# Per-token scalars of two graph layers turned by VectorE and spread by transfers instead of by a TensorE product

## The chip, the cores and the metric

The kernel runs on one core of a Trainium2 chip. A core has a matmul engine (TensorE, PE in the profile; its weight loads are PEld), three engines for elementwise work (VectorE or DVE, ScalarE or ACT, GpSimd or POOL) and SyncE (SP), which only issues transfers here; ScalarE issues some transfers too. Each engine works its own instructions in order and waits for the others by semaphores. The metric is the device time of one launch in microseconds, the median of several runs. Before the change it is 2524.32 us (three runs, 2521.54 to 2528.27).

## The reference

Four graph layers are applied to x, 128 graphs of 64 nodes with 512 features, float32. Each is `x + layer(relu(layernorm(x)))`. Biases, the node mask (all ones) and layers 1 and 2 (attention inside each graph, with one head and with eight) are cut here to what the change meets:

```python
# layer 0
q, k = jnp.split(h @ Wqk, 2, axis=-1)
v = h @ Wv
agg = jnp.einsum('bij,bjd->bid', adj, k)
w = jnp.einsum('bid,bid->bi', q, agg) / jnp.sqrt(512.)    # one scalar a node
x = x + jax.nn.softmax(w, axis=1)[:, :, None] * v         # over the 64 nodes of a graph

# layer 3
Xw = X @ Wv + bv
sj = Xw @ aw[:d, 0]                                       # one scalar a node
si = Xw @ aw[d:, 0]                                       # one scalar a node
e = jax.nn.leaky_relu(sj[:, None, :] + si[:, :, None] + ab[0], negative_slope=0.2)
alpha = A * jnp.exp(e)
transition = alpha / (jnp.sum(alpha, axis=-1, keepdims=True) + 1e-12)
H, Xk = 0, X
for k in range(3):
    H = H + Xk @ Wk[k] + bk[k]
    Xk = jnp.einsum('bij,bjd->bid', transition, Xk)
x = x + relu(H)
```

In both layers a scalar that belongs to a node must be known to all nodes of its graph: w for the softmax, si for the sum with sj. How it gets there is what is changed.

## The kernel before

**Tiles.** A block is 256 tokens, four graphs: two tiles (t = 0, 1) of 128 tokens, one token a partition, two graphs a tile. There are 32 blocks. Every 512x512 product over a block is done with seven products of half-size operands (Strassen's scheme) instead of eight. POOL forms the sums S of the turned input hT (L270 to L274), PE the products (`Product.add`, L299 or L306 in the trace). Products 1 and 6 go first, 5 and 4 second, 2, 7 and 3 late, into two banks, ab and dc. After the first ones ACT keeps p1 and DVE u2 (`keep_ab`, L335 and L336), after the second ACT keeps p5 (`keep_dc`, L344); only then may PE go on in the same bank with the late ones. `store` (L358 to L362) adds it up into the result; the bank is free for the next product when DVE has read it there: ab after L359, dc after L361. In the trace names such as u_y, p_y, ab_y belong to a product y; layer 3 has three, y2 and y1 (the head) and y0 (the tail), and the trace leaves their numbers out.

**Norm.** `norm` (L180) takes DVE's statistics (L185, L186, L188, L189), POOL's rstd and nmr (L191, L193) and ACT's h (L200, two halves, each followed by a transfer to a scratch in DRAM, L204, that ACT issues itself). SP reads it back in another order (L217) and DVE turns it into hT by 32x32 squares (L243).

**The scalars.** In layer 0 DVE's dot (L609) gives w, one value a token, in a column. L616 multiplies an identity of 64 columns by it (wd), so that each row holds w on its own place, and `graph_sums` (L453) multiplies the result by a matrix of two 64x64 blocks of ones on PE (L457): each row of the product, sm_w in PSUM, holds the w of all 64 nodes of its graph. `layer0_end` takes its min (L627), the exponentials on ACT (L633, L638) and updates x (L643). In layer 3 `layer3_dots` does four dots (L915: si and sj, each for two tiles), the multiplication by the identity (L920) and sj (L927); `layer3_in` has the product (sm_i), adds sj (L934), and makes al from it (L940, ACT's exp L941, L943).

**Order.** The program order is written by hand: steps hand lists of closures (`between`) to the places between the first, second and late products, and `tc.issue_after` puts instructions right behind a named one in the order of their own engines. What is issued later on one engine waits behind what is issued earlier.

- Layers 0 and 1 run interleaved, two blocks of layer 0 and two of layer 1 in four steps (the loop over `steps`). `layer0_end` of a block is put in the first slot of the next step, `chore` (L100 to L104, sums of later layers' weights on POOL) in the second.
- Layer 2 runs block by block, fed by `prepare2` and `fetch2`, with the norm and the dots of the first blocks of layer 3 at its end.
- Layer 3 (`layer3_step`): in step b the head does y2 and y1, with the sums and the turn of b + 1 and the norm of b + 2 placed early (behind the last `kept_ab`), `layer3_end` of b - 1 in the second slot (PE's po, L449, then ACT's tz L1013, POOL's L1015, DVE's L1016 and the store of the output), and `layer3_in` of b + 1 in the third. The tail does y0, with den (L966, the row sums of al) and po2, whose results DVE scales at L974 to L977; y0 is stored at L1000 to L1004, and behind its end (`kept`) come the dots of b + 2 and the loads of b + 3.

Of the kernel before, what the change touches and what calls it, by code (L numbers as in the profile page):

```python
# [26 lines left out]
def kernel(ctx: ExitStack, tc: tile.TileContext, a: dict, out: bass.AP):  # L27
# [72 lines left out]
    def chore(n: int = 1):  # L100
        with tc.issue_after(behind[0].ins):
            for _ in range(min(n, len(chores))):
                w, (to, x, y) = chores.pop(0)
                nc.gpsimd.tensor_tensor(w[:, to], w[:, x], w[:, y], ALU.subtract)  # L104
# [63 lines left out]
    eye = const.tile([P, N], FP, tag="eye", name="eye")  # L168
    for g in range(2):
        h = slice(g * N, (g + 1) * N)  # L170
        nc.vector.memset(ones_bd[h, h], 1.0)
        nc.vector.tensor_copy(eye[h, :], ident[h, h])
# [4 lines left out]
    behind_norm, parted = {}, {}  # L177
    read, w2 = [None], []

    def norm(x, name: str, home):  # L180
# [13 lines left out]
        behind_norm.setdefault(0, (by_rows, summed_up))  # L194
        h = med.tile([P, TT, D], FP, tag="h", name=f"h_{name}", bufs=homes["h"])
# [60 lines left out]
    behind = [None]  # L256
# [21 lines left out]
    class Product:  # L278
# [77 lines left out]
        def store(self, y):  # L356
# [4 lines left out]
            nc.vector.tensor_tensor(y[:, 0, F:], self.c, self.u2, ALU.add)  # L361
            nc.gpsimd.tensor_tensor(y[:, 1, F:], self.u3, self.p5, ALU.add)  # L362
# [91 lines left out]
    def graph_sums(e, cols: int, name: str):  # L454

        ps = ps_sc.tile([P, cols], FP, tag="sc", name=f"sm_{name}")
        nc.tensor.matmul(ps, ones_bd, e, start=True, stop=True)  # L457
        return ps

    def reciprocals(e, name: str):  # L460

        den = graph_sums(e.rearrange("p t i -> p (t i)"), TT * N, name)
        r = small.tile([P, TT, N], FP, tag="r", name=f"r_{name}", bufs=2)
        nc.vector.reciprocal(r.rearrange("p t i -> p (t i)"), den)
        return r
# [56 lines left out]
    def setup1():  # L522
# [43 lines left out]
        folded(kt, qt, 1, m, lambda: layer0_end(0, *softmax))  # L566
# [29 lines left out]
    def layer0(b: int, x, adjT, hs, hT, aggs, between):  # L596
# [10 lines left out]
        w = small.tile([P, TT], FP, tag="w", name=f"w_{b}")  # L607
        for t in range(TT):
            nc.vector.scalar_tensor_tensor(  # L609
# [3 lines left out]


        wd = small.tile([P, TT, N], FP, tag="e", name=f"wd_{b}")
        tail[0] = nc.vector.tensor_tensor(  # L616
            wd,
            eye.unsqueeze(1).to_broadcast([P, TT, N]),
            w.unsqueeze(2).to_broadcast([P, TT, N]),
            ALU.mult,  # L620
        )
        return x, gv, w, wd

    def layer0_end(b: int, x, gv, w, wd):
        wrow = graph_sums(wd.rearrange("p t i -> p (t i)"), TT * N, f"w_{b}")
        mn = small.tile([P, TT], FP, tag="mx0", name=f"mn0_{b}")
        nc.vector.tensor_reduce(  # L627
            mn, wrow.rearrange("p (t i) -> p t i", t=TT), AX.X, ALU.min
        )
        nc.vector.tensor_tensor(w, w, mn, ALU.subtract)  # L630
        tot = small.tile([P, TT], FP, tag="tot", name=f"tot_{b}")
        for t in range(TT):
            nc.scalar.activation(  # L633
                wd[:, t, :], wrow[:, t * N : (t + 1) * N], AF.Exp, bias=mn[:, t : t + 1],
                scale=-1.0, accum_out=tot[:, t : t + 1],
            )
# [270 lines left out]
    def layer3_dots(b: int, x, adjT, hs):  # L907
# [3 lines left out]
        sij = small.tile([P, 2, TT], FP, tag="sij", name=f"sij_{b}")  # L911
        for s in range(2):
            for t in range(TT):
                hu = med.tile([P, D], FP, tag="agg", name=f"hu_{b}_{s}_{t}", bufs=2)
                nc.vector.scalar_tensor_tensor(  # L915
                    hu, hs[t], 1.0, us[s], ALU.mult, ALU.mult,
                    accum_out=sij[:, s, t : t + 1],
                )
        di = small.tile([P, TT, N], FP, tag="e", name=f"di_{b}")
        nc.vector.tensor_tensor(  # L920
            di,
            eye.unsqueeze(1).to_broadcast([P, TT, N]),
            sij[:, 1, :].unsqueeze(2).to_broadcast([P, TT, N]),
            ALU.mult,
        )
        sj = small.tile([P, TT], FP, tag="sj", name=f"sj_{b}")
        nc.vector.tensor_scalar(sj, sij[:, 0, :], c3, None, ALU.add)  # L927
        return x, adjT, hs, di, sj

    def layer3_in(b: int, x, adjT, hs, e, sj, made: dict):  # L930


        pi = graph_sums(e.rearrange("p t i -> p (t i)"), TT * N, f"i_{b}")
        nc.vector.tensor_tensor(  # L934
            e,
            pi.rearrange("p (t i) -> p t i", t=TT),
# [188 lines left out]
    for i, (layer, b) in enumerate(steps):  # L1125
        if i == n_steps - 4:
            fetch2(0)
        if i == n_steps - 3:
            fetch2(1)
        if i == n_steps - 1:  # L1130
            fetch2(2)
        between = [[], [lambda: chore(3 if i < 4 else 1)], []]
        if i == 1:
            begun = []
# [18 lines left out]
        elif i + 2 == n_steps:  # L1153
            between[0].append(lambda: prepare2(0))
        else:
            between[0].append(lambda: prepare2(1))
        if layer == 0:
            softmax = layer0(b, *loaded[b], *normed[i], aggs.pop(b, None), between)
            begun = [(0, lambda b=b, softmax=softmax: layer0_end(b, *softmax))]
# [23 lines left out]
    def layer3_step(b: int, ahead: bool = True):  # L1183
# [8 lines left out]
        def begin():  # L1192
# [3 lines left out]
            if b + 2 < n_blk and ahead:  # L1196
                with tc.issue_after(kept_ab[0].ins):
                    normed3 = layer3_norm(b + 2)

        def attention():  # L1200
            if b + 1 < n_blk:
                layer3_in(b + 1, *coming, made_in)

        y = layer3_head(b, ops, [[begin], [ending.pop()], [attention]])
# [7 lines left out]
        if b + 1 == n_blk:  # L1212
            ending[0] = lambda: layer3_last(b, x, al, y, r, y0, ops, kept)
        if b + 2 < n_blk:
            with tc.issue_after(kept.ins):
                if ahead:
                    normed3 = layer3_dots(b + 2, *normed3)
                    fetch3(b + 3)
                else:
                    fetch3(b + 2)  # L1220
# [17 lines left out]
    for b in range(n_blk):  # L1238
        x = loaded2[b][0]
        first_in = lambda: layer3_in(0, *normed3, made_in) if b == n_blk - 2 else None  # L1240
        if b + 1 < n_blk:
            pTs = []
# [5 lines left out]
            def ahead():  # L1248
                with ExitStack() as placed:
                    for i in (pTs[1], kept_c[0], read[0]):  # L1250
                        placed.enter_context(tc.issue_after(i.ins))
                    prepare2(b + 3)
                with tc.issue_after(read[0].ins):
# [121 lines left out]
```

## Time and profile before

One profiled execution, on the same kind of core:

| | us |
|---|---|
| median of three runs | 2524.32 |
| profiled execution, its own time | 2527.11 |
| its span, first to last instruction | 2524.5 |
| PE busy (19488 instructions) | 2487.0 |
| DVE busy (4590) | 1822.0 |
| POOL busy (1710) | 1324.1 |
| ACT busy (2106) | 857.1 |

The time lies 2.6 us above the span, for what lies around it. By time the layers are: the setup to about 110, layers 0 and 1 to about 900, layer 2 to about 1800, layer 3 from there to the end. Most instructions of a group are alike, and a group's row gives their sum and the mean of one. A wait is given as "engine, what it was to do, what it waited for". A busy PE means that matmuls follow each other: the ends of matmuls are modelled, so what a matmul costs is best read from one start to the next.

The transfers that matter here, by their mean time from issue to landing: h to DRAM 2.1 us (256 KB), the parts back 2.8 us (128 KB each), x 3.7 us (512 KB), adjT 2.2 us (64 KB).

### The profile page before, as it was taken

The page shows a single profiled execution, that of the slowest core. Times are in us where ns is not written, and L with a number is a line of the kernel's source. Part 1 is how long each engine was busy: PE and PEld are TensorE (multiplying, and loading weights), DVE is VectorE, ACT ScalarE, POOL GpSimd, SP SyncE. Part 2 cuts the span into 40 slices and gives each one's busy share as a digit, 9 for nine tenths or more (in the row PEclk, how much of TensorE's full clock was granted, in tenths as well). Part 3 has the DMA queues.
Part 4 walks back from the last instruction along what each step waited for, and adds up shares of the span by engine and source line. Part 5 has one row for each costly group of instructions (what it writes and reads, how often), then busy time and mean ns, then how long its engine had stood idle before and what let it go on. Part 6 is the DMA issues. An engine that isn't in the chain of part 4 may idle for free.

```text
span 2524.5 us, 52284 instructions
## 1 busy us (share of the span) xinstructions
PE 2487.0 (99%) x19488; PEld 2124.1 (84%) x19488; DVE 1822.0 (72%) x4590; ACT 857.1 (34%) x2106; POOL 1324.1 (52%) x1710
## 2 busy tenths in 40 slices
PE   9899999999999999999999999999989999999999
PEld 5788888888888888999999999999867777777776
DVE  5577777777777786667667667667568777777775
ACT  3333433333334332333333333333223333333332
POOL 2444343444433445666656556556465555555554
PEclk9999999999999999999999999999999999999999
DMA  7344343333343354443343343344433333333320
GB/s 180 94 127 124 111 127 114 119 107 116 113 126 112 122 156 138 128 133 108 122 132 115 123 131 115 122 136 134 139 112 104 104 103 107 105 106 106 103 77 34
DMA packets 305190, 295.50 MB, mean 117 GB/s; under 512 B 56870, under 2 KB 211494, under 8 KB 304936
## 3 DMA queue, kind: packets, MB, share of 16 engines
q1 hardware_dynamic: 258856, 208.26, 29.2%
q10 hardware_dynamic: 46080, 83.91, 9.1%
q8 instruction: 153, 2.51, 0.4%
q14 instruction: 101, 0.83, 0.1%
HBM read 158.91 MB, written 133.18 MB: 116 GB/s over the span
## 4 chain that ended last, share of the span: by engine, by line
PE 57%; DVE 2%; DMA 1%; POOL 1%; issue 1%; SPq 0%; ACT 0%; POOLq 0%; ACTq 0%; DVEq 0%
PE ab_y L306 13%; PE dc_y L306 9%; PE ab_v L306 4%; PE ab_q L299 4%; PE ab_k L299 4%; PE ab_o L306 4%; PE dc_q L299 3%; PE dc_k L299 3%; PE dc_v L306 3%; PE dc_o L306 3%; PE po L449 2%; PE pc L825 1%; PE s L750 1%; DVE hu L915 1%; DMA x<-x 0%
## 5 line engine op out<-in xcount | busy, mean ns | idle before, releaser
L200 ACT ACTIVATE h<-x,nmr,rstd 128x512 f32<-128x512 f32 x256 | 194.8, 806 | 207.6 <-POOL nmr L193 202.1
L270 POOL TENSOR_TENSOR S<-hT 128x256 f32<-128x256 f32 x128 | 97.8, 764 | 243.9 <-DVE hT L243 231.1
L306 PE MATMUL ab_y<-L_Wk,hT 128*128 128x256 f32 x768 | 204.9, 389 | 7.9 <-DVE u_y L336 6.7
L306 PE MATMUL ab_v<-L_Wv,hT 128*128 128x256 f32 x768 | 201.0, 384 | 3.7 <-DVE u_v L336 3.0
L306 PEld LDWEIGHTS ab_y<-L_Wk,hT 128*128 128x128 f32 x768 | 138.7, 190 | 74.9 <-DVE u_y L336 30.7
L191 POOL TENSOR_TENSOR rstd<-ve,neghalf 128x2 f32<-128x2 f32 x128 | 90.5, 707 | 209.2 <-DVE mv L189 190.7
L306 PE MATMUL dc_v<-L_Wv,S 128*128 128x256 f32 x768 | 198.0, 380 | 0.7 <-ACT p_v L344 0.7
L306 PE MATMUL ab_y<-L_Wk,S 128*128 128x256 f32 x768 | 198.0, 380 | 0.0
L306 PE MATMUL ab_v<-L_Wv,S 128*128 128x256 f32 x768 | 197.1, 379 | 0.0
L306 PE MATMUL dc_y<-L_Wk,S 128*128 128x256 f32 x768 | 193.5, 380 | 0.1
L243 DVE STREAM_TRANSPOSE hT<-part 128x512 f32<-128x512 f32 x252 | 174.4, 698 | 8.6 <-DMA part<-h_rows 5.9
L306 PEld LDWEIGHTS dc_y<-L_Wk,S 128*128 128x128 f32 x768 | 146.0, 191 | 21.3 <-issue 0.8
L306 PEld LDWEIGHTS ab_y<-L_Wk,S 128*128 128x128 f32 x768 | 146.5, 191 | 20.1
L185 DVE BATCH_NORM_STATS2 stats<-x 128x6 f32<-128x512 f32 x256 | 162.8, 677 | 0.0
L306 PEld LDWEIGHTS ab_v<-L_Wv,S 128*128 128x128 f32 x768 | 145.9, 190 | 19.8
L306 PEld LDWEIGHTS dc_v<-L_Wv,S 128*128 128x128 f32 x768 | 143.8, 191 | 20.0 <-ACT p_v L344 0.9
L306 PEld LDWEIGHTS ab_v<-L_Wv,hT 128*128 128x128 f32 x768 | 138.2, 190 | 21.9 <-DVE u_v L336 4.0
L915 DVE SCALAR_TENSOR_TENSOR hu<-h,us 128x512 f32<-128x512 f32 x128 | 139.4, 1139 | 1.9 <-POOL bs L894 1.4
L1015 POOL TENSOR_TENSOR tz<-tz,y 128x512 f32<-128x512 f32 x62 | 90.4, 1458 | 95.4 <-ACT tz L1013 95.3
L336 DVE TENSOR_TENSOR u_v<-ab_v,p_v 128x256 f32<-128x256 f32 x96 | 40.4, 421 | 126.4 <-ACT p_v L335 125.9
L1016 DVE SCALAR_TENSOR_TENSOR x<-tz,x 128x512 f32<-128x512 f32 x62 | 42.9, 692 | 112.3 <-POOL tz L1015 112.3
L272 POOL TENSOR_TENSOR S<-hT,S 128x256 f32<-128x256 f32 x128 | 113.0, 883 | 0.0
(257 smaller groups left out, 6181.7 us busy)
## 6 DMA issues: line engine op xcount, KB each, us to landing
x<-x SPq DMA_DIRECT2D x128, 512.0 KB, 3.8
h_rows<-h ACTq DMA_DIRECT2D x252, 256.0 KB, 2.1
part<-h_rows SPq DMA_DIRECT2D x504, 128.0 KB, 2.8
x<-in_x_dram SPq DMA_DIRECT2D x32, 512.0 KB, 3.7
e_rows<-et ACTq DMA_DIRECT2D x64, 256.0 KB, 3.0
pT<-e_rows SPq DMA_DIRECT2D x128, 128.0 KB, 3.1
out_dram<-x SPq DMA_DIRECT2D x31, 512.0 KB, 2.8
adjT<-in_adjT_dram SPq DMA_DIRECT2D x64, 64.0 KB, 2.2
```

Source lines behind the costliest of these rows:

```text
L185: nc.vector.bn_stats(stats[:, t, :], x[:, t, :])
L191: nc.gpsimd.tensor_tensor(rstd, ve, neghalf, ALU.pow)
L200: nc.scalar.activation(hs[t], x[:, t, :], AF.Relu, bias=nmr[:, t : t + 1], scale=rstd[:, t : t + 1])
L243: nc.vector.transpose(hT[:, :, t * P : (t + 1) * P].rearrange("p k (g q) -> p g k q", q=Q), part[:, t * 4 : (t + 1) * 4].rearrange("p g (k ...
L270: nc.gpsimd.tensor_tensor(S1, A21, A22, ALU.add)
L272: nc.gpsimd.tensor_tensor(S4, A12, S2, ALU.subtract)
L299: nc.tensor.matmul(dst[:, m * P : (m + 1) * P], w[:, place, k, m * P : (m + 1) * P], left[:, k, :], start=key not in self.begun, stop=last ...
L306: nc.tensor.matmul(dst, left[:, k, :], w[:, place, k, :], start=key not in self.begun, stop=last and k == 1, skip_group_check=True,)
L449: nc.tensor.matmul(ps[t][half[g ^ t]], e[half[g], t, :], us[t][half[g]], start=True, stop=True)
L915: nc.vector.scalar_tensor_tensor(hu, hs[t], 1.0, us[s], ALU.mult, ALU.mult, accum_out=sij[:, s, t : t + 1],)
L1015: nc.gpsimd.tensor_tensor(tz[t], tz[t], y0[:, t, :], ALU.add)
L1016: nc.vector.scalar_tensor_tensor(x[:, t, :], tz[t], 0.0, x[:, t, :], ALU.max, ALU.add)
```

## The change

The identity, the two multiplications by it (L616, L920) and `graph_sums` are taken out. In their place the column of scalars is written into a 128x32 tile that is zero elsewhere (two of them, by turns); DVE turns it by 32x32 squares, so that the scalars lie in rows; SP writes these rows to a scratch in DRAM (two transfers) and reads them back to all 64 partitions of each graph (two transfers).

```diff
-    def graph_sums(e, cols: int, name: str):
-
-        ps = ps_sc.tile([P, cols], FP, tag="sc", name=f"sm_{name}")
-        nc.tensor.matmul(ps, ones_bd, e, start=True, stop=True)
-        return ps
...
+    def spread(pair, name: str):
+
+        row = tc.dram_tile([TT, P], FP, name=f"{name}_row")
+        lines = small.tile([P, Q], FP, tag="lines", name=f"{name}_lines", bufs=2)
+        nc.vector.transpose(lines, pair)
+        for t in range(TT):
+            nc.sync.dma_start(
+                row[t : t + 1].rearrange("o (s q) -> (o s) q", q=Q), lines[t::Q]
+            )
+        to = small.tile([P, TT, N], FP, tag="e", name=name)
+        by_graph = row.rearrange("(o t) (g i) -> g o t i", o=1, g=2)
+        for g in range(2):
+            spread_out[0] = nc.sync.dma_start(
+                to[half[g]], by_graph[g].to_broadcast([N, TT, N])
+            )
+        return to
```

The users read this tile in SBUF instead of the product in PSUM, and later:

```diff
 # layer 0
-        wd = small.tile([P, TT, N], FP, tag="e", name=f"wd_{b}")
-        tail[0] = nc.vector.tensor_tensor(
-            wd,
-            eye.unsqueeze(1).to_broadcast([P, TT, N]),
-            w.unsqueeze(2).to_broadcast([P, TT, N]),
-            ALU.mult,
-        )
-        return x, gv, w, wd
+        return x, gv, w, spread(pair, f"w_of_{b}")
...
-        wrow = graph_sums(wd.rearrange("p t i -> p (t i)"), TT * N, f"w_{b}")
-        nc.vector.tensor_reduce(
-            mn, wrow.rearrange("p (t i) -> p t i", t=TT), AX.X, ALU.min
-        )
+        nc.vector.tensor_reduce(mn, wd, AX.X, ALU.min)
...
-            begun = [(0, lambda b=b, softmax=softmax: layer0_end(b, *softmax))]
+            def end0(b=b, softmax=softmax):
+                with tc.issue_after(stored[1].ins):
+                    layer0_end(b, *softmax)
+
+            begun = [(3, end0)]
 # layer 3
+        di = spread(pair, f"si_of_{b}")
+        nc.vector.tensor_scalar(sj, sj, c3, None, ALU.add)
...
-        pi = graph_sums(e.rearrange("p t i -> p (t i)"), TT * N, f"i_{b}")
         nc.vector.tensor_tensor(
             e,
-            pi.rearrange("p (t i) -> p t i", t=TT),
+            e,
             sj.unsqueeze(2).to_broadcast([P, TT, N]),
             ALU.add,
         )
...
             if b + 2 < n_blk and ahead:
-                with tc.issue_after(kept_ab[0].ins):
+                with tc.issue_after(kept_ab[0].ins), tc.issue_after(spread_out[0].ins):
                     normed3 = layer3_norm(b + 2)
 
         def attention():
-            if b + 1 < n_blk:
-                layer3_in(b + 1, *coming, made_in)
-
-        y = layer3_head(b, ops, [[begin], [ending.pop()], [attention]])
+            layer3_in(b + 1, *coming, made_in)
+
+        y = layer3_head(b, ops, [[begin], [ending.pop()]])
...
+        if b + 1 < n_blk:
+            with tc.issue_after(kept.ins):
+                attention()
         if b + 2 < n_blk:
             with tc.issue_after(kept.ins):
                 if ahead:
                     normed3 = layer3_dots(b + 2, *normed3)
-                    fetch3(b + 3)
+                    with tc.issue_after(read[0].ins):
+                        fetch3(b + 3)
```

So in layer 0 the min, the exponentials and the update of x are issued behind the store of the second product of the next step. In layer 3 the sum with sj and what follows it moves from between the late products of the head to the end of the step before, ahead of the dots; and the norm of b + 2 is issued behind the spread of the scalars of the block before it.

The rest concerns order alone. POOL's weight sums are also placed behind the first product's store and behind the latest norm:

```diff
-        between = [[], [lambda: chore(3 if i < 4 else 1)], []]
+        between = [[], [
+            lambda: chore(3 if i < 4 else 1, (stored[0], normalised[0]) if i else ())
+        ], [], []]
```

At the seam from layer 1 to 2, x of the first three blocks of layer 2 is loaded in steps n - 6, n - 4 and n - 2 (it was n - 4, n - 3 and n - 1), and `prepare2` of blocks 0 and 1 is placed behind the last dot of layer 0. At the seam from layer 2 to 3, the norms and dots of blocks 0 and 1 of layer 3 are placed in earlier places of layer 2's blocks n - 3 and n - 2, the last block's attention weights are turned and `layer3_in` of block 0 is issued right behind the output product of block n - 2, the loads of x of layer 3 are issued earlier, and the biases later:

```diff
+        if b == n_blk - 2:
+            with tc.issue_after(read[0].ins):
+                fetch3(2)
+                fetch3(3)
+            with tc.issue_after(of_o.taken.ins):
+                pTs = layer2_turned(b + 1, es)
+                layer3_in(0, *normed3_0, made_in)
+            with tc.issue_after(read[0].ins):
+                bias3 = biases3()
```

## The prediction

> **What bounds the kernel now.** I read the busy time of the engines by stretch of the span first, because a mean over four layers hides where there is room. Columns: the stretch in us, its length, then the busy us (and instructions) of TensorE (PE), weight loads, VectorE (DVE), ScalarE (ACT), GpSimd (POOL), then the granted clock, DMA share, GB/s.
>
> ```profile
> 0.00:110.00 110.00, 95.92 (x399) 67.36 (x400) 59.66 (x152) 38.89 (x87) 39.27 (x60) 0.97 0.57 148
> 110.00:860.00 750.00, 746.70 (x5305) 640.14 (x5305) 558.22 (x1498) 285.98 (x747) 312.96 (x461) 1.00 0.39 116
> 1740.00:1900.00 160.00, 148.58 (x1259) 125.69 (x1258) 106.46 (x257) 44.83 (x111) 96.16 (x118) 0.97 0.42 126
> 1900.00:2500.00 600.00, 600.00 (x3161) 475.45 (x3160) 469.86 (x1192) 189.98 (x398) 347.96 (x399) 1.00 0.30 97
> ```
>
> PE has no gap in layer 3 (1900 to 2500), 3.3 us in layers 0 and 1; 14.1 us are idle in the start-up and 11.4 us in the seam from layer 2 to 3. So an edit gains only if PE gets less to do or if those two stretches are mended, and any new lateness in layer 3 is paid in full. PE's waits say what the idle time waited for (us in total, times, longest):
>
> ```profile
> PE ab_y L306 <- DVE u_y L336: 6.7, 2, 6.5
> ...
> PE sm_w L457 <- DVE wd L616: 4.5, 2, 3.9
> PE ab_g L306 <- DVE u_g L336: 3.9, 2, 3.2
> ...
> PE pc L825 <- DMA pT<-e_rows: 2.8, 2, 1.7
> ```
>
> The 6.5 us lie at 1844.8 and the 1.7 at 1817.6 (seam); the 3.9 at 80.4 and 3.2 at 90.9 (start-up).
>
> **Removed matmuls.** The groups that the change takes from PE:
>
> ```profile
> L457 PE MATMUL sm_w<-wd,ones_bd 128*128 128x128 f32 x64 | 12.5, 277 | 4.5 <-DVE wd L616 4.5
> L457 PE MATMUL sm_i<-di,ones_bd 128*128 128x128 f32 x64 | 12.4, 275 | 0.0
> ```
>
> One call is two of these records. Ends on PE are modelled, so I take what a call moves the next matmul by: sm_i starts at 2131.41 and the next at 2131.64, about 0.22 us. That is 32 x 0.22 = 7.0 us in layer 0 and 7.0 in layer 3, 14 us if nothing else changes.
>
> **Layer 3, the part that decides.** I compare the instruction order of both builds in one steady step, block 15, with this timeline of before (start, us, engine, line, operation):
>
> ```profile
> 2116.47 1.28 DVE L185 BATCH_NORM_STATS2 stats<-x 128x6 f32<-128x512 f32 x2
> ...
> 2116.87 0.29 PE L966 MATMUL den<-ones_bd,al 64*64 64x1 f32 x8
> ...
> 2118.24 2.27 DVE L977 SCALAR_TENSOR_TENSOR y<-po,r,y 128x512 f32<-128x512 f32 x3
> ...
> 2119.34 1.52 ACT L200 ACTIVATE h<-x,nmr,rstd 128x512 f32<-128x512 f32 x2 [1.91 <-POOL nmr L193]
> ...
> 2123.06 0.90 DVE L915 SCALAR_TENSOR_TENSOR hu<-h,us 128x512 f32<-128x512 f32 x1
> ...
> 2127.63 0.74 DVE L336 TENSOR_TENSOR u_y<-ab_y,p_y 128x256 f32<-128x256 f32 x2
> ...
> 2128.72 1.13 PE L306 MATMUL ab_y<-L_Wk,hT 128*128 128x256 f32 x4
> 2128.82 2.09 ACT L1013 ACTIVATE tz<-po,r 128x512 f32<-128x512 f32 x3 [0.59 <-PE po L449]
> ...
> 2130.89 0.69 DVE L1016 SCALAR_TENSOR_TENSOR x<-tz,x 128x512 f32<-128x512 f32 x1 [2.51 <-POOL tz L1015]
> ...
> 2133.35 0.42 DVE L359 TENSOR_TENSOR u_y<-ab_y,p_y 128x256 f32<-128x256 f32 x1
> ...
> 2134.23 1.03 PE L306 MATMUL ab_y<-L_Wk,hT 128*128 128x256 f32 x4
> ```
>
> The next den is at 2137.78, so a step is 20.91 us. Before, the norm of a later block (L185 on DVE, h on ACT) lies right behind den, early in the step, with ACT free for it. In the changed build the same norm is placed behind the spread of the scalars, and so behind the four dots. On DVE the order from L1004 is: L934, a dot, L940, two dots, L943, the last dot, sj, the 32x32 turn, L185 twice, then L336 of y2 and y1, L188, L189, L1016, then L359. On ACT h and its two DMA issues now stand ahead of tz (L1013). Queued behind them: tz, then POOL's L1015, DVE's L1016 and behind it L359, whose result frees the bank for PE's first product of y0. Counted from den (2116.87 = 0):
>
> 1. L977 began at 1.37, straight behind the norm. Without it, it needs den, L974, L975 and the first po, about 0.8. Gain 0.57: L934 may start at 6.19 - 0.57 = 5.62 (the dots' old place, 2123.06).
> 2. L934, L940, L943 come ahead of the last dot: 0.28 + 0.29 + 0.29 = 0.86. Four dots from 2123.06 to 2127.30: 4.24. sj 0.13. The turn of a 128x32 tile is not in this trace: at least L975's 0.14 (128x2), at most L243's 0.71 (128x512, sixteen times as many elements); it is nearest the small one, I take 0.2. The removed L920 (0.2 by starts) came behind sj and is not in the sum any more. End: 11.05.
> 3. L185 twice 1.28, one aggregate 0.12, L336 0.42: 12.87. PE wanted this at 2128.72, 11.85: late by 1.0.
> 4. Second aggregate and second L336: L188 at 13.3. From L188 to h it was 1.28 (2118.06 to 2119.34): h at 14.6, its two halves 1.52, and 0.35 until the second issue is out (2120.86 to 2121.21): tz at 16.45, where it was 11.95.
> 5. tz to L1016 2.07, L1016 0.69, L359 0.42, 0.1 to PE: the first product of y0 at 19.7. It stood at 17.36, or 17.14 without the sm_i. PE's lateness from step 3 is inside this, not added.
> 6. From there to the next den 3.55: 23.25 a step against 20.91, +2.3.
>
> Bounds: with dots at the pace of the same operation beside an idle POOL (L609, 0.68 from start to start) step 2 is 1.5 shorter and the sum +0.8; with the turn at 0.71 it is +2.9. POOL's sums still run beside the dots, so I stay near the sum with **+2.2**. The pattern holds for 28 of the 32 steps: 28 x 2.2 = +61.6 (22 to 81). The other four save 0.22 each: -0.9.
>
> **The clock.** The granted clock fell to a half for about 3.4 us behind three pairs of gaps or single gaps in this trace: 3.9 us (80.4), 3.2 us (90.9), and 1.7 followed by 1.1 within 2.5 us (1817.6 to 1820); 1.6 alone (954.6) did not. The new stalls, 1.0 and 1.6 some 5 us apart, lie between. I take nothing, and up to 1.7 x 28 = 48 us as a rival. The Trainium skill, "TensorE: Matmul & The Clock Gate", section "HAM oscillation — how this bites in real kernels", asks only for no gap over about 3.4 us; by that the stalls would cost no clock, and neither should the 3.2 us gap have, which did; the row decides.
>
> **Layers 0 and 1.** -7.0 for the matmuls. The min (L627), exp and x update move a step later, behind the store of the second product: the transfers have some 10 us there, against two landings of 2.8 (the part<-h_rows row) or at worst 6.3 (a 0.5 KB load in the start-up), so they are covered; without that cover each step would wait 2 to 3 us. But L627 now sits ahead of L699's reciprocals, which were ready just in time for PE (575.70), 0.2, and the x update (L643, 2.5 us of DVE with what belongs to it) ahead of a norm, whose h leads to u_v at 586.8, 0 to 0.6. I count 0.1 for the second: 0.3 x 15 groups of four steps = 4.5, at most 12, at least 0. Net **-2.5** (-7 to +5). The 256 small DMAs (8 a block, or four a turn) queue on SP; part transfers behind them have 2 us or more before hT, and PE's waits show none that goes back to a part: nothing, at most 0.5 a step if they were late.
>
> **Start-up.** POOL's weight sums (L104, 2.49 us at 83.75) stand ahead of rstd (86.19), and h, p_g, u_g and PE's 3.2 us follow; the others (to 76.5) stand ahead of gv, L609 and the 3.9 us wait of sm_w. They move behind the store and the norm, and sm_w is gone. Of 7.1 us of waits and 3.4 of half clock, part comes back, since the norm now follows the x update: **-7** (0 to -10).
>
> **Seams.** Into layer 3 the last block's e is turned earlier (2.8 us of pc waits) and dots are drawn forward (6.5 us at 1844.8). Into layer 2, PE's 3.2 us. I take **-6** of the 11.4 + 3.2 us idle (and 1.7 of half clock at 1820); 0 to -14.
>
> **Sum.** 61.6 - 0.9 - 2.5 - 7 - 6 = +45. The profiled execution has a span of 2524.5 and took 2527.1, 2.8 above the median 2524.3; the sum goes on both alike: 2572 for that execution, **2569 us** for the median.
>
> **Rivals.** *Layer 3 keeps its pace (faster).* One mechanism: DVE reaches L185 so early that tz is not held. It must give back 2.3 of the 2.3: dots at 0.68 give 1.5, the three small instructions in gaps 0.5. Below +0.55 a step the kernel is faster, since the rest brings 16.4. At +0.3: 8.4 - 16.4, 2516; at no stall 2524.3 - 7.0 - 2.5 - 13 = 2502. For it: DVE is 78% busy there, so there are gaps. Against it: the dots read 1139 ns in the mean beside POOL, and L185 is behind the last of them in any case. *Only step 3 bites:* tz hidden, +1.0 - 0.2 a step: 22 - 16.4, 2530. Against: ACT takes tz strictly behind h. *The clock falls too:* 2569 + 48 = 2617. *Transfers late on SP*, 0.5 a step in layers 0 and 1 and in layer 3: 2569 + 32 = 2601. That the matmuls stay is excluded: the changed build has none.
>
> **Chances.** Forecast 0.68; layer 3 keeps its pace 0.19; only step 3 0.06; clock 0.04; SP 0.03. About 0.3% (7.6 us) is what a measurement can tell from no change: faster 0.19, within 0.04 (where the first two rivals meet), slower 0.77. The forecast's own range is 2530 to 2590 (22 to 81 in layer 3); for 8 in 10 it reaches down to 2517, leaving out most of the first rival, and above 2592 clock and SP.
>
> **What would show it.** In the profile after: den to den in layer 3 of 23 us (20.7 if wrong); PE waits of ab_y on u_y of L336 (1.0) and L359 (1.6 or so), some 28 of each; tz starting 16 us behind den with ACT's h just before it; PE idle of 60 to 70 us between 1900 and the end; no 3.9 and 3.2 us waits in the start-up. A tz right behind po, or dots under 0.8, would make the forecast wrong.

## The result, and the profile after

The changed kernel takes 2611.22 us (median of four runs, 2609.53 to 2612.85) against 2523.24 (four runs of the kernel before): a ratio of 1.0345, with an interval of 1.0327 to 1.0363. It is 88 us slower where 45 were forecast. (Spans differ by 84.2: the profiled execution before was among the slower ones.) The direction and the place were forecast, the size was not.

The profiled span is 2608.7 us (2524.5 before). Busy time by stretch, same columns as before:

```profile
0.00:110.00 110.00, 99.03 (x440) 70.41 (x441) 63.89 (x165) 41.18 (x91) 41.98 (x65) 1.00 0.58 150
110.00:860.00 750.00, 736.14 (x5205) 630.13 (x5204) 540.39 (x1480) 287.01 (x744) 304.57 (x456) 1.00 0.39 118
1740.00:1900.00 160.00, 155.33 (x1292) 129.96 (x1290) 108.36 (x269) 46.73 (x116) 98.91 (x123) 0.99 0.39 118
1900.00:2500.00 600.00, 528.68 (x2689) 402.00 (x2690) 420.24 (x1050) 163.84 (x347) 285.22 (x349) 1.00 0.30 93
```

PE has 71 us without work in 600 us of layer 3, where it had none. The granted clock stayed at 1.00 there. The start-up and the seam lost idle time, layers 0 and 1 gained some. PE's waits:

```profile
PE ab_y L307 <- DVE u_y L360: 30.5, 28, 1.8
PE ab_y L307 <- DVE mv L186: 29.6, 27, 1.3
PE dc_y L307 <- DVE y L362: 21.3, 29, 1.9
PE ab_v L307 <- DVE u_v L337: 16.5, 16, 2.3
...
PE den L692 <- ACT gT L380: 3.8, 1, 3.8
```

Most lines up to L928 are one to some twenty higher than in the kernel before (L307 was L306, L337 was L336, L360 was L359, L923 was L915); L934 to L1016 are the same. Each of the first three waits comes once a step of layer 3. The second names L186, the last thing that the profile saw end on DVE; what PE needs is the L337 that runs just ahead of it, as the step itself shows. One steady step of layer 3, from den to den:

```profile
2122.71 0.29 PE L966 MATMUL den<-ones_bd,al 64*64 64x1 f32 x8
...
2123.95 2.28 DVE L977 SCALAR_TENSOR_TENSOR y<-po,r,y 128x512 f32<-128x512 f32 x3 [0.49 <-PE po L450]
...
2133.82 0.20 DVE L471 STREAM_TRANSPOSE si_of_lines<-pair 128x32 f32<-128x32 f32 x1
2133.95 1.24 DVE L185 BATCH_NORM_STATS2 stats<-x 128x6 f32<-128x512 f32 x2
...
2135.19 0.39 DVE L337 TENSOR_TENSOR u_y<-ab_y,p_y 128x256 f32<-128x256 f32 x1
...
2135.73 1.10 PE L307 MATMUL ab_y<-L_Wk,hT 128*128 128x256 f32 x4 [1.10 <-DVE mv L186]
...
2137.14 1.52 ACT L201 ACTIVATE h<-x,nmr,rstd 128x512 f32<-128x512 f32 x2 [3.07 <-POOL nmr L193]
...
2139.06 2.09 ACT L1013 ACTIVATE tz<-po,r 128x512 f32<-128x512 f32 x3 [0.40 <-ACT h L201]
...
2139.82 3.11 POOL L1015 TENSOR_TENSOR tz<-tz,y 128x512 f32<-128x512 f32 x2 [2.72 <-ACT tz L1013]
...
2141.12 0.69 DVE L1016 SCALAR_TENSOR_TENSOR x<-tz,x 128x512 f32<-128x512 f32 x1 [5.00 <-POOL tz L1015]
2141.73 0.42 DVE L360 TENSOR_TENSOR u_y<-ab_y,p_y 128x256 f32<-128x256 f32 x1
...
2142.20 1.13 PE L307 MATMUL ab_y<-L_Wk,hT 128*128 128x256 f32 x4 [1.06 <-DVE u_y L360]
2142.90 0.72 POOL L363 TENSOR_TENSOR y<-u_y,p_y 128x256 f32<-128x256 f32 x1
...
2142.97 1.20 DVE L1016 SCALAR_TENSOR_TENSOR x<-tz,x 128x512 f32<-128x512 f32 x1 [0.82 <-POOL tz L1015]
...
2144.42 0.41 DVE L362 TENSOR_TENSOR y<-dc_y,u_y 128x256 f32<-128x256 f32 x1
...
2144.89 1.13 PE L307 MATMUL dc_y<-L_Wk,S 128*128 128x256 f32 x4 [0.69 <-DVE y L362]
```

The next den is at 2146.81: 24.10 us a step, where it was 20.91. The chain is the one that was forecast (norm behind the dots, h ahead of tz on ACT, tz ahead of L1015, L1016 and L360), with one member more at the end: the second L1016, which also waits for POOL, stands ahead of L362, and PE's dc_y waits for that. This L1016 also took longer, 1.20 us where it took 0.69 before; POOL's L363 had begun 0.07 us ahead of it. In the kernel before:

```profile
2132.74 0.69 DVE L1016 SCALAR_TENSOR_TENSOR x<-tz,x 128x512 f32<-128x512 f32 x1 [1.16 <-POOL tz L1015]
```

Where the time went follows from the first and last starts of PE's groups (from the views by tile; the differences are worked out):

| from | to | before | after | difference |
|---|---|---|---|---|
| start | first ab_g of layer 1 | 112.5 | 105.8 | -6.7 |
| first ab_g | last ab_g (layers 0 and 1) | 838.5 | 846.4 | +7.9 |
| last ab_g | first ab_q of layer 2 | 10.0 | 13.4 | +3.4 |
| first ab_q | last ab_q (layer 2) | 846.7 | 845.6 | -1.1 |
| last ab_q | first den of layer 3 | 52.2 | 40.5 | -11.7 |
| first den | last den (layer 3) | 652.3 | 744.6 | +92.3 |

Of the 92.3 us, 89.4 lie in the 28 steady steps (3.19 each) and 3.1 in the first step of layer 3, which took 29.87 us from den to den, 26.77 before.

### The profile page after: what moved, and what is told of

It reads as the page before. It is cut to its first block, busy times and chain, and to the rows that moved or that the text cites. A ratio compares the mean times of both kernels' runs of the same rounds, so it can differ in the third digit from the quotient of the medians.

```text
span 2608.7 us, 52510 instructions
## 1 busy us (share of the span) xinstructions
PE 2488.6 (95%) x19360; PEld 2103.8 (81%) x19360; DVE 1815.9 (70%) x4588; ACT 857.7 (33%) x2106; POOL 1294.8 (50%) x1712
## 4 chain that ended last, share of the span: by engine, by line
PE 63%; DVE 18%; POOL 7%; issue 5%; ACT 5%; DMA 1%; ACTq 1%; DVEq 0%; SPq 0%; POOLq 0%
PE ab_v L307 11%; PE dc_v L307 7%; PE ab_k L300 4%; PE ab_q L300 4%; PE ab_o L307 4%; DVE hu L923 4%; PE ab_g L307 3%; PE dc_q L300 3%; PE dc_k L300 3%; PE dc_o L307 3%; PE dc_y L307 3%; PE dc_g L307 3%; ACT tz L1013 2%; PE ab_g L300 2%; POOL tz L1015 2%
## 5 line engine op out<-in xcount | busy, mean ns | idle before, releaser
L307 PE MATMUL ab_y<-L_Wk,hT 128*128 128x256 f32 x768 | 206.4, 391 | 61.5 <-DVE u_y L360 30.5
L307 PEld LDWEIGHTS ab_y<-L_Wk,hT 128*128 128x128 f32 x768 | 138.1, 189 | 141.0 <-issue 54.2
L191 POOL TENSOR_TENSOR rstd<-ve,neghalf 128x2 f32<-128x2 f32 x128 | 91.9, 718 | 312.3 <-DVE mv L189 293.3
L307 PE MATMUL ab_v<-L_Wv,hT 128*128 128x256 f32 x768 | 202.5, 386 | 17.6 <-DVE u_v L337 16.5
L307 PE MATMUL dc_y<-L_Wk,S 128*128 128x256 f32 x768 | 196.4, 384 | 21.9 <-DVE y L362 21.3
L307 PE MATMUL dc_v<-L_Wv,S 128*128 128x256 f32 x768 | 197.5, 379 | 0.6 <-ACT p_v L345 0.6
L307 PE MATMUL ab_v<-L_Wv,S 128*128 128x256 f32 x768 | 197.1, 379 | 0.0
L307 PE MATMUL ab_y<-L_Wk,S 128*128 128x256 f32 x768 | 197.1, 379 | 0.0
L307 PEld LDWEIGHTS dc_y<-L_Wk,S 128*128 128x128 f32 x768 | 143.3, 190 | 52.9 <-DVE y L362 32.9
L1016 DVE SCALAR_TENSOR_TENSOR x<-tz,x 128x512 f32<-128x512 f32 x62 | 57.6, 929 | 173.4 <-POOL tz L1015 173.4
L307 PEld LDWEIGHTS ab_v<-L_Wv,hT 128*128 128x128 f32 x768 | 138.0, 190 | 38.9 <-DVE u_v L337 20.7
L185 DVE BATCH_NORM_STATS2 stats<-x 128x6 f32<-128x512 f32 x256 | 164.5, 673 | 5.3 <-DMA x<-in_x_dram 5.3
L307 PEld LDWEIGHTS ab_y<-L_Wk,S 128*128 128x128 f32 x768 | 145.9, 190 | 19.8
L307 PEld LDWEIGHTS ab_v<-L_Wv,S 128*128 128x128 f32 x768 | 145.9, 190 | 19.8
L307 PEld LDWEIGHTS dc_v<-L_Wv,S 128*128 128x128 f32 x768 | 143.3, 190 | 19.7 <-issue 0.8
L337 DVE TENSOR_TENSOR u_v<-ab_v,p_v 128x256 f32<-128x256 f32 x96 | 40.7, 424 | 148.4 <-ACT p_v L336 146.6
L1015 POOL TENSOR_TENSOR tz<-tz,y 128x512 f32<-128x512 f32 x62 | 92.2, 1488 | 95.1 <-ACT tz L1013 91.1
L336 ACT COPY p_y<-ab_y 128x256 f32<-128x256 f32 x96 | 35.7, 372 | 289.1 <-DVE si_of L934 164.3
L923 DVE SCALAR_TENSOR_TENSOR hu<-h,us 128x512 f32<-128x512 f32 x128 | 120.1, 957 | 0.8 <-ACT h L201 0.8
```

The lines of the kernel that those rows point to most:

```text
L185: nc.vector.bn_stats(stats[:, t, :], x[:, t, :])
L191: nc.gpsimd.tensor_tensor(rstd, ve, neghalf, ALU.pow)
L307: nc.tensor.matmul(dst, left[:, k, :], w[:, place, k, :], start=key not in self.begun, stop=last and k == 1, skip_group_check=True,)
L337: self.kept = nc.vector.tensor_tensor(self.u2, self.b, self.p1, ALU.add)
L923: nc.vector.scalar_tensor_tensor(hu, hs[t], 1.0, us[s], ALU.mult, ALU.mult, accum_out=(pair if s else sj)[:, t : t + 1],)
L1015: nc.gpsimd.tensor_tensor(tz[t], tz[t], y0[:, t, :], ALU.add)
```

## The experiments

All times are medians beside runs of the kernel before on the same chip (2523.2 to 2525.9). The order on DVE and ACT that is told of is that of the built kernels.

**Which edit of layer 3 makes the order.** The prediction read that the norm stands behind the spread because it is placed behind `spread_out`. That is a transfer, though, and `issue_after` puts only instructions of the same engine behind it, here SP's reads of the parts. The other new edge on SP is that of the load of x. The final order of one engine's instructions is chosen when the kernel is built, within the edges that are given. The runs below suggest that it follows when each can be expected to be ready; how the builder reckons this, no run shows.

```diff
 # e1: the changed kernel without the edge on the load
-                    with tc.issue_after(read[0].ins):
-                        fetch3(b + 3)
+                    fetch3(b + 3)
```

> The changed kernel, with one edge taken out: the load of x of block b+3 in layer 3 no longer queues on SP behind the part reads of the norm of b+2. That alone puts L185 of the norm back ahead of L977 and h well ahead of tz; the spread, its turn and L934 to L943 ahead of the dots stay. Theory (the late load makes the scheduler put the norm behind the dots, and that order makes the stalls): den to den 20.7 to 20.9 us in layer 3 where the changed kernel has 24.1; 2611 - 92 = 2519 us, 2510 to 2528. Rival (the spread and the three small operations ahead of the dots are the cost): a step stays above 23, 2580 or more.

2516.24 us (2515.59 to 2516.75), ratio 0.996, 0.9945 to 0.9975. A step takes 20.68 us (den at 2110.22 and 2130.90); the chain of layer 3, first to last den, is 648.7 us. Of PE's waits in layer 3 only two single ones are left:

```profile
PE ab_v L307 <- DVE u_v L337: 16.9, 16, 2.3
...
PE dc_y L307 <- DVE y L362: 1.9, 1, 1.9
PE ab_y L307 <- DVE u_y L337: 1.1, 1, 1.1
```

L185 now stands ahead of den, h runs right behind it and tz right behind po, though L934 to L943 still stand ahead of the last dot:

```profile
2109.35 1.27 DVE L185 BATCH_NORM_STATS2 stats<-x 128x6 f32<-128x512 f32 x2
...
2110.22 0.29 PE L966 MATMUL den<-ones_bd,al 64*64 64x1 f32 x8
...
2112.69 1.52 ACT L201 ACTIVATE h<-x,nmr,rstd 128x512 f32<-128x512 f32 x2 [1.91 <-POOL nmr L193]
...
2122.17 2.09 ACT L1013 ACTIVATE tz<-po,r 128x512 f32<-128x512 f32 x3 [0.59 <-PE po L450]
```

So two lines of the diff cost 95 us, and without them the kernel is faster than before. In a steady step the spread itself costs nothing: a step is 0.23 us shorter than before, which is what the removed matmul took (0.22). From the first to the last den only 3.6 of some 6.5 us are gained, as the first step is 2.4 longer than before; both waits of layer 3 listed above lie in it.

```diff
 # e2: the changed kernel without the other edge
-                with tc.issue_after(kept_ab[0].ins), tc.issue_after(spread_out[0].ins):
+                with tc.issue_after(kept_ab[0].ins):
                     normed3 = layer3_norm(b + 2)
```

> The changed kernel, with the other edge taken out: the part reads of layer 3's norm no longer queue on SP behind the spread's transfers. The order on DVE and ACT stays the changed kernel's. Theory: no difference, 2611 within 8 us. Rival (parts late behind the spread on SP are what delays the step): 20 us or more faster.

2611.02 us (2610.25 to 2613.63): no difference. The edge that the prediction named does nothing to the time, and DVE's order is the same (L185 at 2133.39, right behind the turn at 2133.26).

**The order, or the landing of x.** In the changed kernel the load of x is issued at 2120.53 and L185 of that x starts at 2133.95, with no wait ahead of it. To be sure, e3 loads early and keeps the order:

```diff
 # e3: e1, and L185 kept behind the spread's turn on DVE
-        nc.vector.transpose(lines, pair)
+        turned_pair[0] = nc.vector.transpose(lines, pair)
...
-                with tc.issue_after(kept_ab[0].ins), tc.issue_after(spread_out[0].ins):
+                with tc.issue_after(turned_pair[0].ins), tc.issue_after(spread_out[0].ins):
                     normed3 = layer3_norm(b + 2)
```

> x of layer 3 is loaded early as in e1, but an edge on DVE keeps L185 behind the spread's turn, so the order on DVE and ACT is the changed kernel's again. Theory (the order costs, not when x lands): 2611 within 8 us, the same three waits of PE (u_y L337 and L360, y L362) of about 1 us a step. Rival (L185 waits for a load that lands late): about as fast as e1, 2519.

2611.91 us (2611.28 to 2613.64), and the same waits:

```profile
PE ab_y L307 <- DVE u_y L360: 32.1, 29, 1.7
PE ab_y L307 <- DVE mv L186: 29.5, 27, 1.3
PE dc_y L307 <- DVE y L362: 21.3, 29, 1.9
```

The load costs nothing by itself. Its place on SP's queue changes the order on DVE and ACT (e1), and the order makes the stalls (e3). That x looks late to the builder is the likely link; it is inferred.

**h ahead of tz alone.** e4 has the statistics early as in e1, but h of the norm is issued between the last p5 and tz:

```diff
 # e4: e1, and h apart from the statistics of the norm
+        def apply():
+            with tc.issue_after(spread_out[0].ins), tc.issue_after(kept_c[0].ins):
+                for act in put_off:
+                    act()
+            with tc.issue_after(last_h[0].ins) if put_off else nullcontext():
+                end_before()
...
-        y = layer3_head(b, ops, [[begin], [ending.pop()]])
+        y = layer3_head(b, ops, [[begin], [apply]])
```

> e1 with the statistics early, but h of the norm on ACT right ahead of tz, behind the last p5 (L345). h could then start at 11.4 after den, as soon as that p5 is done, so tz starts at 13.3 (16.35 in the changed kernel, 11.95 before) and PE's first y0 product is free at 16.6, before it is wanted at 17.1; the second L1016 and L362 may hold dc_y by 0.3. Theory (h ahead of tz costs only because the statistics are late): as e1 to 14 us slower, 2519 to 2533. Rival (tz behind h costs its own 1.9 us a step wherever it stands): 2519 + 28 x 1.5 = 2561 or more.

2520.76 us (2518.84 to 2523.79), 4.5 us above e1.

```profile
2120.85 1.52 ACT L209 ACTIVATE h<-x,nmr,rstd 128x512 f32<-128x512 f32 x2
...
2122.77 2.09 ACT L1021 ACTIVATE tz<-po,r 128x512 f32<-128x512 f32 x3 [0.40 <-ACT h L209]
```

The den of this step is at 2109.59: tz starts at 13.2 instead of 12.0 (e1: 2122.17 behind 2110.22), and that is nearly all slack. In these runs, standing ahead of tz is dear only when h itself is late, at 14.4 behind den.

**The late load in the kernel before.**

```diff
 # e8: the kernel before, one edge added in layer3_step
-                    fetch3(b + 3)
+                    with tc.issue_after(read[0].ins):
+                        fetch3(b + 3)
```

> The kernel before, with nothing but the changed kernel's edge on the load of x of block b+3 in layer 3. L185 of the norm then stands behind the four dots and h between p5 and p5 ahead of tz, with no spread, no turn and no moved L934. Theory (this edge alone makes the loss): a step of 22.5 to 23.5 where it was 20.9, 2525 + 28 x 2.1 = 2584 us, 2565 to 2600. Rival (it takes the spread and the moved sum too): 2535 or less.

2603.28 us (2602.08 to 2603.95), ratio 1.0308, 1.0293 to 1.0324: 78 us from one edge, without any part of the spread. The expectation was too low again. The first wait has another name here: the matmul of the scalars, sm_i, waits until ACT has read po (tz):

```profile
PE sm_i L457 <- ACT tz L1013: 39.2, 28, 1.4
PE ab_y L306 <- DVE u_y L336: 19.4, 29, 6.1
PE dc_y L306 <- DVE y L361: 8.3, 28, 0.3
```

The order is again that of the changed kernel: L185 behind the dots, h 13.7 and tz 15.9 behind den. A step is 23.68 us.

```profile
2122.48 0.29 PE L966 MATMUL den<-ones_bd,al 64*64 64x1 f32 x8
...
2133.16 1.27 DVE L185 BATCH_NORM_STATS2 stats<-x 128x6 f32<-128x512 f32 x2
...
2136.20 1.52 ACT L200 ACTIVATE h<-x,nmr,rstd 128x512 f32<-128x512 f32 x2 [3.24 <-POOL nmr L193]
...
2138.39 2.10 ACT L1013 ACTIVATE tz<-po,r 128x512 f32<-128x512 f32 x3
```

**Layers 0 and 1.** PE's 16 waits for u_v (16.9 us in e1) come, from 243.9 on, once in each group of four steps, 0.96 us each time but the last. e5 moves `layer0_end` of every second block behind the next norm's statistics:

```diff
 # e5: e1, and the end of odd blocks of layer 0 in the next step but one
+            def end0_behind_norm(b=b, softmax=softmax):
+                with tc.issue_after(measured[0].ins):
+                    layer0_end(b, *softmax)
...
+            between[0].extend(held.pop(i, ()))
```

> e1, with layer0_end of the second block of each pair one place later: behind the statistics of the next norm (L189), which it stands ahead of in the changed kernel with its min and its update of x (L649). Theory (these 2 to 3 us of DVE ahead of the norm make h, p_v and u_v late, PE's 16 waits of about 1.0 in layers 0 and 1): the waits go, 2516 - 15 = 2501 us, 2497 to 2507. Rival (ACT or the landing of the transfers holds u_v, or the update now standing ahead of u_v holds it instead): 2513 to 2520.

2513.99 us (2513.02 to 2514.93), 2 us less than e1, not 15. The wait goes on in two parts of about 0.3: the exponentials now stand ahead of p_g on ACT, the update of x ahead of u_v on DVE.

```profile
PE ab_v L307 <- DVE u_v L337: 8.7, 15, 2.3
PE dc_g L300 <- ACT p_g L349: 5.1, 12, 1.2
```

e9 puts the same end one place further, behind u_v on DVE and behind p5 on ACT:

```diff
 # e9, against e5
-                with tc.issue_after(measured[0].ins):
+                with tc.issue_after(kept_ab[0].ins), tc.issue_after(kept_c[0].ins):
                     layer0_end(b, *softmax)
...
-            between[0].extend(held.pop(i, ()))
+            between[1].extend(held.pop(i, ()))
```

> e5, with layer0_end of the second block one place later still: on DVE behind u_v (L337), on ACT behind p_v and p5 of the second product, so that neither the update of x nor the exponentials stand ahead of what PE waits for. Theory (what is left in e5 is that same lateness at the next place: 0.3 + 0.3 us twice in each of 15 groups): the waits of ab_v and dc_g go, 2514 - 11 = 2503 us, 2499 to 2508. Rival (the DVE work only moves on to gT or to the reciprocals and PE waits there): 2511 or more.

2514.22 us (2512.81 to 2515.01), no better: the update of x (1.97 us there) now stands ahead of gT.

```profile
PE pa L450 <- DVE gT L376: 10.0, 12, 1.0
PE ab_v L307 <- DVE u_v L337: 5.1, 3, 2.3
```

The rival held both times. At three places in this part of the group the update only changes which wait PE has. e7 takes the spread out of layer 0 and keeps it in layer 3:

```diff
 # e7: e1, layer 0 by the identity and the matmul, ended in the first slot
...
-            begun = [(3, end0)]
+            begun = [(0, lambda b=b, softmax=softmax: layer0_end(b, *softmax))]
```

> e1 with layer 0's scalars by the identity and the matmul again, ended in the first slot of the next step as before; layer 3 with the spread, one pair tile and one tile of lines instead of two. Theory (in layers 0 and 1 the spread gives back 15 us for 7 saved): 2516 - 15 + 7 = 2508, to 2514 if the start-up's wait for wd comes back. Rival (removing the matmuls is a gain there too): 2520 or more.

2513.25 us (2509.06 to 2513.35), 3 us less than e1. From layer 1's first ab_g (110.6) to its last (949.4) it is 838.8 us, 7.8 less than e1's 846.6 (106.6 to 953.2), and the start-up gives 4.0 back. So in layers 0 and 1 the spread, with the later end of layer 0 that goes with it, is a loss, in the start-up a gain.

**Start-up and seam.** e11 is the kernel before with only the new order of POOL's weight sums:

```diff
 # e11: the kernel before
...
-        between = [[], [lambda: chore(3 if i < 4 else 1)], []]
+        between = [[], [
+            lambda: chore(3 if i < 4 else 1, (stored[0], normalised[0]) if i else ())
+        ], []]
```

> The kernel before with nothing but the changed order of POOL's weight sums in layers 0 and 1 (behind the first product's store and the latest norm). The prediction's step for the start-up (the sums hold gv and rstd, and with them 7.1 us of PE's waits and 3.4 of half clock): 2 to 7 us faster, 2525 - 5 = 2520. Rival (the start-up gained only because sm_w left PE): no difference, 2523 to 2527.

2523.50 us (2520.38 to 2524.91), ratio 0.9988, 0.9979 to 0.9997: 1.6 us, which lies in the rival's range. Its first ab_g stands at 111.0, where the changed kernel has 105.8; most of the gain of the start-up is therefore not from this order alone. In e11 the waits of sm_w are gone, but one of ab_g for u_g has grown from 3.2 to 4.1 us (88.3); e7 has the same (86.4), the changed kernel has not. Whether that is because the matmul is gone or because `layer0_end` comes later, no run separates.

e6 moved POOL's last two weight sums of layers 0 and 1 into layer 2, against the 3.8 us wait of den for gT at 960.9:

```diff
 # e6, against e5
-            lambda: chore(3 if i < 4 else 1, (stored[0], normalised[0]) if i else ())
+            lambda: chore(
+                3 if i < 4 else 1 if i < n_steps - 2 else 0,
+                (stored[0], normalised[0]) if i else (),
+            )
...
-        [lambda: prepare2(2), chore], [ends[n_blk - 1], chore], [lambda: turned2(1)]
+        [lambda: prepare2(2), lambda: chore(2)], [ends[n_blk - 1], lambda: chore(2)],
+        [lambda: turned2(1)]
```

> e5, with POOL's last two weight sums in layers 0 and 1 moved from their last two steps into the first block of layer 2. They stand ahead of rstd of layer 2's second norm in the changed kernel, and PE waits 3.8 us at 960.9 (den behind gT). Theory: that wait goes, 2 to 4 us less than e5. Rival (PE only waits for something else at the seam): no difference from e5.

2514.60 us (2513.38 to 2516.33): no difference from e5, and the wait stayed (3.7 us), because POOL's sums came to stand in nearly the same place. What holds gT is ACT: h of layer 2's third block stands ahead of it and waits for POOL's nmr, which stands behind those sums. e10 is e9 with that norm behind layer 1's last copy and store:

```diff
 # e10, against e9
...
+    def prepare2_behind():
+        with tc.issue_after(copied[0].ins), tc.issue_after(stored[0].ins):
+            prepare2(2)
+
     qk, ops = layer2_in(0, normed2[0], [
-        [lambda: prepare2(2), chore], [ends[n_blk - 1], chore], [lambda: turned2(1)]
+        [prepare2_behind, chore], [ends[n_blk - 1], chore], [lambda: turned2(1)]
```

> e9, with the norm of layer 2's third block on ACT behind the last copy of layer 1's v and on POOL behind its store. In the changed kernel h of that norm stands ahead of gT (L380) on ACT, and rstd, which waits for POOL's weight sums, ahead of h: PE waits 3.8 us at 960.9. Theory: that wait goes, 3 to 4 us less than e9. Rival (PE then waits for layer 2's first products instead): no difference.

2509.80 us (2509.15 to 2510.03), 4.4 below e9, and that wait is gone, with the 3.4 us at half clock that followed it in e9 (960.8).

**A version faster than both.** e12 joins what gained: layer 3 by the spread with the early load, blocks 0 and 1 of layer 0 by the spread, the other blocks by the matmul, and e10's placement at the seam.

```diff
 # e12, against e7
+        by_spread = b < 2
+        if by_spread:
+            pair = column_pair()
+            w = pair[:, :TT]
...
+        if by_spread:
+            return x, gv, w, spread(pair, f"w_of_{b}")
...
-            begun = [(0, lambda b=b, softmax=softmax: layer0_end(b, *softmax))]
+            begun = [(3 if b < 2 else 0, end0)]
```

> e7, with the spread in layer 0 for blocks 0 and 1 alone (the matmul from block 2 on), and the norm of layer 2's third block placed as in e10. Theory (by PE's marks e7 is 4 us slower than e1 up to layer 1's first product and 7.6 faster over layers 0 and 1; e10's placement takes 3.8 at the seam): 2513 - 4 - 4 = 2505 us, 2502 to 2508. Rival (the start-up's gain or layer 0's does not stand beside the other): 2509 or more, no better than e10.

2502.76 us (2500.96 to 2504.24), ratio 0.9908, 0.9892 to 0.9925: 23 us below the kernel before. PE's largest waits are then of one to three times each:

```profile
PE tw_q L505 <- DMA q<-in_L_Wqk_dram: 4.7, 1, 4.7
PE ab_g L309 <- DVE u_g L339: 3.6, 3, 1.7
PE ab_v L309 <- DVE u_v L339: 2.5, 2, 1.3
```

## Why the prediction was wrong in size

- **Layer 3, steps 1 to 5: right, in part by luck.** Behind den, predicted and measured: end of the turn 11.05 and 11.31, end of the first L337 12.87 and 12.87, h 14.6 and 14.43, tz 16.45 and 16.35, first product of y0 19.7 and 19.49. The late L337 stalls PE by 1.10 (1.0 predicted). The turn took 0.20, as taken between its bounds. Three terms were too small: L977 began at 1.24 instead of 0.8, behind the last of po and not behind its first half, and L934 and L940 took 0.53 and 0.80 where 0.28 and 0.29 were taken. The last two dots, at 0.68 instead of 1.06, made up for most of that.
- **Layer 3, step 6: this failed.** "From there to the next den 3.55" took PE's part of a step over unchanged. Measured it is 4.61 (2142.20 to 2146.81), because L362 stands behind the second L1016, which waits for POOL's second L1015 and then takes 1.20, and PE's dc_y waits 0.69 for it; by starts this product comes 0.86 later, and two others are 0.1 longer each. The chain was followed to the first product that it delays and not to the second. The 1.06 us a step are 30 us over 28 steps, of which the earlier first product (19.49) takes back 6. Choosing 2.2 where the sum said 2.3 took off another 4, and the first step of layer 3, for which nothing was taken, brought 3 more. Together they are the gap between 60.7 forecast for layer 3 and 92.3 measured.
- **The reason for the order: wrong**, though it did not enter the sum. The order was read from the built kernel; it was put down to the edge behind the spread, which e2 shows to do nothing. The prediction does not speak of the diff's line on the load of x. On the chip that load is issued 13.4 us ahead of its L185 and holds nothing, but it is the line that sets the order (e1, e3, e8).
- **Layers 0 and 1: too small.** Net -2.5 was taken, +7.9 measured. The place was named (the update of x ahead of the norm, u_v late, "0 to 0.6"), and the measured wait is 0.95 in nearly every group. It lies outside the bounds of that term, of which only 0.1 was taken. The 0.2 for L627 ahead of the reciprocals shows as a single wait of 0.5. (The row of 6.3 us that is called a load there, c_row<-c, is of stores; nothing rests on it.)
- **Start-up: right in size**, -6.7 against -7, but not for the reason that was put first: e11 shows 1.6 us for the order of the sums, and e7, with the matmul and the early end back in layer 0, loses 4.0 of it.
- **Seams: better than forecast**, -9.4 against -6 with layer 2 counted in: -11.7 into layer 3, +3.4 into layer 2, a new wait that the prediction did not see (h of layer 2's third norm ahead of gT). No run takes the seam into layer 3 apart. Its idle time of 11.4 us was not all there was to gain: around the 6.5 us wait the clock stood at half from 1842.4 to 1849.2 in the kernel before, which the prediction's list of such stretches leaves out, and in the changed kernel there is no such stretch at that seam. The longer first step of layer 3 gives 3.1 us back.
- **The clock: right in the steady steps.** Stalls of 1.10, 1.06 and 0.69 within 10 us cost no granted clock (1.00 from 1900 to 2500), so no 48 us came on top. Two other places of the changed kernel did cost it, 3.4 us at half clock each: behind the 3.8 us wait at 960.9, and in the first step of layer 3 behind waits of 1.4 and 1.9 us (1871.7 and 1878.4). The rule of the Trainium skill ("TensorE: Matmul & The Clock Gate", section "HAM oscillation — how this bites in real kernels"), no gap over about 3.4 us, agrees with the steady steps and with the 3.8 us wait; it does not explain the 3.2 us gap of the kernel before, nor the 1.4 and 1.9 us here, behind which the clock fell too.
- **The rival "layer 3 keeps its pace"** is what e1 makes of the kernel: 20.68 us a step, 2516 us. It gets there by an early norm ahead of the dots, not by faster dots, which the rival counted on. (Its point of no change is 16.4 / 28 = 0.59 us a step, not 0.55; nothing rests on that either.)

## What to carry to other kernels

A load's place on a transfer queue can cost much more than its landing: if the order of the other engines is chosen by when data can be expected, an edge on the queue reorders engines that it does not touch, so compare the orders of two builds with and without each edge. When a chain of waits ends at a product, follow it through every later product of the step that needs the same engine, not only to the first that is late. Small work taken from a full engine is a gain only if the work that replaces it finds a place: in layer 3 it did, in layers 0 and 1 each place tried delayed something that PE waits for.

## What was not expected of the hardware

The same dot (128x512) took 1.21 us beside POOL's sums and 0.68 us when POOL was idle, within one step of the changed kernel:

```profile
2129.14 0.77 POOL L275 TENSOR_TENSOR S<-hT 128x256 f32<-128x256 f32 x1
2129.25 1.22 DVE L923 SCALAR_TENSOR_TENSOR hu<-h,us 128x512 f32<-128x512 f32 x1
...
2129.88 1.17 POOL L1005 TENSOR_TENSOR y<-y,bs 128x256 f32<-128x256 f32 x1
...
2130.39 0.80 DVE L940 SCALAR_TENSOR_TENSOR si_of<-si_of 128x128 f32<-128x128 f32 x1
...
2131.01 0.77 POOL L273 TENSOR_TENSOR S<-hT,S 128x256 f32<-128x256 f32 x1
...
2131.12 1.21 DVE L923 SCALAR_TENSOR_TENSOR hu<-h,us 128x512 f32<-128x512 f32 x1
...
2132.26 0.68 DVE L923 SCALAR_TENSOR_TENSOR hu<-h,us 128x512 f32<-128x512 f32 x1
```

Its mean fell from 1139 ns to 957, although its inputs and shape stayed, because two of the four dots of a step came to stand where POOL is idle. L940, 128x128 from and to SBUF, rose from 316 to 756 ns in the mean when it was moved to where POOL works.

What counts in these rows is which of the two began first. Of the 128 dots of the changed kernel, the 65 that began while a POOL instruction was running took 1.1 us or more, the 63 others 0.68 to 0.69. Of its 62 L1016, the 29 that began behind a running L363 of POOL took 1.2 us; the other 33 took 0.69, though in 31 of them a POOL instruction began before they ended. Not every POOL instruction does this: beside the two-column L191 and L193 the update of x (L649) kept its 0.75 us. A place on DVE thus has a price that depends on what POOL does at that time, and an edit that moves an instruction changes both.
